# A two-layer graph attention kernel: fifteen-product thirds for the second products, seven-product aggregation for the last head and layer 2, and sums forked in PSUM

## The chip, the cores and the metric

The kernel runs on one core of a Trainium2 chip. Time is the device time of one execution in microseconds; lower is better. The engines have queues of their own: PE (TensorE, the matrix engine), DVE (VectorE), ACT (ScalarE), POOL (GpSimd) and SP (SyncE). SP issues plain transfers, POOL issues the transfers that add what they bring to what already lies in the destination; 16 DMA engines carry both. Each engine works through its queue in order and waits on semaphores of the others.

## The reference, cut to what matters

512 nodes, 768 features, 16896 edges with both directions and the self loops; layer 1 has 8 heads of 768 features, layer 2 has one head.

```python
h = (x @ W).reshape(n, H, C)                     # W1: 768 x 6144, W2: 6144 x 768
e = leaky_relu(alpha_s[src] + alpha_d[dst], 0.2)  # alpha = <h, a>
e = exp(e - max over dst); alpha = e / (sum over dst + 1e-16)
out = segment_sum(h[src] * alpha)                 # concatenated over heads, + b
...
h = elu(gat_layer(x, W1, ...)); out = gat_layer(h, W2, ...)
return layernorm(x + out)
```

The kernel writes the edges as a dense 512 x 512 matrix of counts. A head of layer 1 is then three dense products in fp32: the projection hs = x W1[:, head] (512 x 768 x 768), the aggregation gT = elu((PT hs) + b) (512 x 512 x 768, PT being the normalised attention), and the second product, which adds g W2[head] (512 x 768 x 768) into h2, the layer-2 features. After the eighth head come layer 2's attention, its aggregation of h2 and the norm.

## The kernel before, in words

**Products.** One `nc.tensor.matmul` has a 128 x 128 weight and a moving operand of up to 512 columns; in fp32 it is two PE instructions. The kernel saves PE work with block schemes that need fewer products than the plain method and pay for it with additions on DVE:

- Seven products for a 2 x 2 x 2 split (`left`, `right`, `projection`, `second`): 42 matmuls of 384 columns for a projection or a second product. `mixed` does the same for an aggregation: 42 matmuls of 256 columns.
- Fifteen products for a 2 x 3 x 3 split (`by_thirds`, with `load_thirds` and `x_thirds` for the operands): 60 matmuls of 256 columns. Before the change only the projections of heads 3 to 7 use it.

The sums of the left operand are made on DVE (`gsums`, `left_sums`, `x_thirds`), those of the right operand partly on DVE, partly by transfers of the POOL queue with `accum_op=ALU.add`.

**Stages.** The loop `for h in range(H - 1)` runs, in this order: `mixed(h)` (aggregation and elu of head h), `second(h)`, and the projection of head h + 2. The attention scores of head h + 1 (`lift`, `leak`, `rank`, `weigh`, `turn_out`, `turn_in`) are worked in between the products of `second(h)`. The last head is aggregated plainly, by `aggregate`: 24 matmuls of 512 columns. Layer 2 is aggregated plainly too, in the last loop: for each block of 128 nodes 4 matmuls of each column group, with the norm of a block done while the next one is multiplied.

**Order.** The program keeps the order in which the Python calls are written. So what stands where in each engine's queue is set by these loops by hand: `pairs[n][0]()` multiplies, `pairs[n][1]()` empties the PSUM bank, and sums and scores are called between them. PSUM: five banks in a ring `mm` (`Ring`), two for transposes, one for broadcasts.

**Loads.** W1[h + 2] goes to the buffers named `w2...` at the head of the loop body. W2[h + 1] goes to the buffers named `w1...` at the end of `second(h)`, right behind `reload_x()`, which brings five sums of x back from DRAM:

```python
if not last and n == 6:
    turn_out(q[3], 3, weigh(q[3], 3, scale=False))
    if 0 < h:
        sums = rest_of_thirds()
        reload_x()
    load_w2(h + 1)()
```

`load_w2` loads t1 (half of the upper rows), adds the other half to it, loads six blocks of rows, and adds the lower right block to the upper right one; the DVE sums from it (lines 384 and 385) come after the last product of the following projection.

Of the kernel before, what the change touches and what calls it, by code (L numbers as in the profile page):

```python
# [18 lines left out]
EPS_DEN = 1e-16  # L19
# [18 lines left out]
def gat_pass(  # L38
# [56 lines left out]

    mm, held = Ring(banks[:3]), Ring(banks[3:])
# [22 lines left out]
    def load_w(W, h, slot, m):  # L119


        t1 = wpool.tile([P, HK, HALF], F32, name=f"{slot}t1")
        upper = m[:HK * P, :].rearrange("(k p) d -> p k d", p=P)
        nc.sync.dma_start(t1, upper[:, :, L])
        nc.gpsimd.dma_start(t1, upper[:, :, R], accum_op=ALU.add)
        if slot == "w2":
            rows_ = wpool.tile([P, DC, D], F32, name="w2r")
            W[h] = [rows_[:, :HK], rows_[:, HK:], t1]
        else:
            W[h] = [wpool.tile([P, HK, D], F32, name=f"{slot}{r}") for r in range(2)] + [t1]  # L130
        for k in range(DC):
            nc.sync.dma_start(W[h][k // HK][:, k % HK, :], m[k * P:(k + 1) * P, :])

        def rest():

            nc.gpsimd.dma_start(W[h][0][:, :, R], m[HK * P:, R].rearrange("(k p) d -> p k d", p=P),
                                accum_op=ALU.add)
        return rest
# [3 lines left out]
    def third(rows_, k, n):  # L142
        return rows_[:, 2 * k:2 * k + 2, n * TH:(n + 1) * TH]

# [3 lines left out]
    def load_thirds(h):  # L148

        m = w1[:, h * D:(h + 1) * D]  # L150

        def part(k, n):
            return m[k * TH:(k + 1) * TH, n * TH:(n + 1) * TH].rearrange("(k p) d -> p k d", p=P)

        def flat(j):
            return wpool.tile([P, HK, HALF], F32, name=f"w2t{j}").rearrange("p k n -> p (k n)")

        rows_, pair_ = wpool.tile([P, DC, D], F32, name="w2r"), flat(1)
        add = ALU.add
        for k in range(DC):  # L160
# [8 lines left out]
        raw = {(k, n): third(rows_, k, n) for k in range(3) for n in range(3)}  # L169
# [33 lines left out]
    W1[0] = [wpool.tile([P, HK, D], F32, name=f"w1{r}") for r in range(2)]  # L203
# [231 lines left out]
    def by_thirds(h, A_, B_):  # L435

        HS[h] = hs = hpool.tile([P, NT, D], F32, name="hs")
# [6 lines left out]
        def step(p, chain, o, how):  # L444
# [9 lines left out]
            def empty():  # L454
# [3 lines left out]
                else:  # L458
                    nc.vector.tensor_tensor(out(o), out(o), ps, op=how)  # L459
            return multiply, empty  # L460

        plus, minus = ALU.add, ALU.subtract
        return [step(*a) for a in (
# [4 lines left out]
            ("P3", "y", (0, 2), -1.0))]  # L468

    def second(h, A_, B_):  # L470
# [3 lines left out]
        def pair(p, i, start, acc, new):  # L474
            def multiply(between=None):
                if start:
                    bank[i] = mm.next()
                product(bank[i], A_, B_, p, i, start, between)

            def empty():  # L480
                a, ps = acc(i), bank[i][:, :HALF]
                if new and h == 0 and p in ("P1", "P2"):
                    nc.scalar.copy(a, ps)
                elif new and (h == 0 or h == H - 1 and p == "P1"):
                    nc.vector.tensor_scalar(a, ps, -1.0 if p == "P7" else 1.0, None, op0=ALU.mult)
                else:
                    nc.vector.tensor_tensor(a, a, ps, op=ALU.subtract if p == "P7" else ALU.add)  # L487
            return multiply, empty

        steps = [  # L490
            ("P1", True, lambda i: u2[:, i, :], True),
            ("P2", False, lambda i: h2[:, i, L], True),
            ("P6", True, lambda i: u2[:, i, :], False),
            ("P7", True, lambda i: h2[:, 2 + i, R], True),
            ("P4", False, lambda i: h2[:, 2 + i, L], True),
            ("P5", True, lambda i: h2[:, 2 + i, R], False),
            ("P3", False, lambda i: h2[:, i, R], True),
        ]
        return [pair(p, i, *rest) for p, *rest in steps for i in range(2)]
# [13 lines left out]
    nb1T = const.tile([P, H * DC], F32, name="nb1T")  # L513

# [98 lines left out]
    def turn_b1():  # L613
# [3 lines left out]
        nc.scalar.activation(nb1T, psb[:, :H * DC], AF.Copy, scale=-1.0)  # L617

# [9 lines left out]
    if not general:  # L628
# [35 lines left out]
        def digits():  # L664

            whole = ohp.tile([P, NT, SW], I32, name="whole")
            nc.vector.tensor_scalar(whole, sums[:, :NT * SW].rearrange("p (t c) -> p t c", c=SW), float(1 << 24), None,
                                    op0=ALU.min)
            for d in range(N // SW):
# [3 lines left out]
                else:  # L673
                    nc.vector.tensor_scalar(o, whole, 3 * d, None, op0=ALU.logical_shift_right)

# [4 lines left out]
        s1, s2, s3, s4 = xsums  # L680
        m = lambda n: items[n][0]()
        e = lambda n: items[n][1]()
        hot = [f for q_ in range(NT) for f in one_hots(q_)]

        def some_hot(n):
            for f in hot[:n]:
                f()
            del hot[:n]

        some_hot(3)  # L690
        m(0)
        turn_x(2, 0)
        turn_x(3, 0)
        e(0)
        e(1)
        turn_x(2, 1)
        turn_x(3, 1)
        m(2)
        m(3)
        some_hot(2)  # L700
        s1()
        B1 = weight_sums()
        e(2)
        s2()
        e(3)
        s4()
        some_hot(1)
        m(4)
        m(5)
        e(4)  # L710
        wsums[0]()
        m(6)
        e(5)
        m(7)
        e(6)
        e(7)
        s3()
        some_hot(3)
        count((0, 1))
        m(8)  # L720
        some_hot(1)
        m(9)
        e(8)
        wsums[1]()
        e(9)
        turn_b1()
        m(10)
        m(11)
        some_hot(1)
        e(10)  # L730
        some_hot(1)
        e(11)
        m(12)
        halves = [half_logits(0, t) for t in range(NT)]
        ours, theirs = ([p_[j] for p_ in halves] for j in range(2))
        for f in (ours[0], theirs[0], ours[1]):
            f()
        count((2, 3))
        m(13)
        digits()  # L740
        e(12)
        e(13)
        ours[2]()
        for t in range(2):
            logarithm(t, counts)
        ours[3]()
        pairs = first_projection(1, XA, B1, lambda: spread(0))
        pairs[0][0]()
        masks(0)
        fold_count(0)  # L750
        q = [lift(0, 0)]
        theirs[1]()
        for t in range(2, NT):
            logarithm(t, counts)
        warm = small.tile([P, 1], F32, name="warm")
        nc.scalar.activation(warm, tiny, AF.Exp)
        q.append(lift(0, 1))
        for n in (0, 1):
            pairs[n][1]()
        for t in (2, 3):  # L760
            theirs[t]()
            q.append(lift(0, t))
    else:
# [28 lines left out]
        q = [lift(0, t) for t in range(NT)]  # L792
# [11 lines left out]
    def weigh(q, t, scale=True):  # L804
# [3 lines left out]
        nc.vector.tensor_scalar(rden, den, EPS_DEN, None, op0=ALU.add)  # L808
# [50 lines left out]
    def left_sums(h):  # L859
        hs = HS[h]  # L860
        a11, a12, a21, a22 = hs[:, :2, L], hs[:, 2:, L], hs[:, :2, R], hs[:, 2:, R]
        s1, s2, s4 = (gS.rearrange("p a k n -> p a (k n)")[:, j, :].rearrange("p (k n) -> p k n", k=2)
# [20 lines left out]
    def mixed(h, A_, B_, fill):  # L883

        tt = nc.vector.tensor_tensor
        behind = []

        def some(n):
            for f in fill[:n]:
                f()  # L890
            del fill[:n]

        for c in range(HK):
            u = work.tile([P, HN], F32, name="u")
            w = work.tile([P, HN], F32, name="w")
            zr = work.tile([P, N], F32, name="zr", bufs=3)
            bank = {}

            def part(p, over=None):
                if over is None:  # L900
                    bank[p] = mm.next()
                else:
                    bank[p] = bank[over]
                for k in range(2):
                    nc.tensor.matmul(bank[p][:, :HN], A_[p][:, k, c * P:(c + 1) * P], B_[p][:, k, :],  # L905
                                     start=over is None and k == 0, stop=k == 1, skip_group_check=True)
                return bank[p][:, :HN]

            nc.scalar.copy(u, part("P1"))  # L909
            if behind:  # L910

                behind = behind[0]()
            tt(u, u, part("P6"), op=ALU.add)
            tt(w, u, part("P7"), op=ALU.add)
            for f in behind[:1]:
                f()
            near_l = elu(h, c, part("P2", over="P1"), near, "l")
            some(1)
            tt(zr[:, far_], part("P5"), w, op=ALU.subtract)
            for f in behind[1:]:  # L920
                f()
            tt(zr[:, near], u, part("P4", over="P7"), op=ALU.add)
            near_l()
            tt(u, part("P3", over="P5"), u, op=ALU.subtract)
            some(-(-len(fill) // (2 * (HK - c) - 1)))
# [413 lines left out]
```

## Time and profile before

| | |
|---|---|
| median of 3 runs | 631.49 us (631.09 to 631.51) |
| the profiled execution | 631.3 us, of which the span from first to last instruction is 629.5 us |
| PE busy | 620.2 us (99%) |
| DVE busy | 491.1 us (78%) |
| ACT busy | 289.1 us (46%) |
| POOL busy | 62.2 us (10%) |
| granted TensorE clock | 0.998 |
| moved by DMA | 107.49 MB |

A row of the groups gives the line of the kernel, the engine, the operation, output and inputs by tile name, the shapes, the count, then busy time and mean duration of one, then the idle time of the engine before these instructions and what ended it. A row of the chain in order of time gives start, length, engine, tile, line and count. PE durations overlap their neighbours; the chain's rows, length over count, give the distance from one start to the next. SP's and POOL's rows show when a transfer is issued; "us to landing" is from issue to landing.

### The profile page before, as it was taken

Reading aid. Unit: us, or ns where it says so; the run is one execution under the profiler, and the core shown is the slowest. Engines: PE = TensorE matmul, PEld = TensorE weight load, DVE = VectorE, ACT = ScalarE, POOL = GpSimd, SP = SyncE. Lnnn points to the kernel's source line nnn. Section 1 sums busy time; section 2 is a strip of 40 time slices with the busy share of each in tenths; the row PEclk is TensorE's granted clock in tenths of the full one; section 3 lists DMA queues with packets and bytes.
Section 4 is the critical chain, followed back from the end, with each engine's and each line's share of the span. In section 5 each row is a group of like instructions: output and inputs, shape, how many; then the busy total and the mean of one; then the engine's idle time right before and its main releaser. Section 6 shows DMA issues by size and latency. Waiting matters only on the chain.

```text
span 629.5 us, 7475 instructions
## 1 busy us (share of the span) xinstructions
PE 620.2 (99%) x2509; PEld 435.5 (69%) x2509; DVE 491.1 (78%) x986; ACT 289.1 (46%) x511; POOL 62.2 (10%) x105
## 2 busy tenths in 40 slices
PE   9999999999999999999999999999999999999995
PEld 5665675558658885688758886688757886545553
DVE  8889878787887877777876878678876878676775
ACT  3138684703556073723546164722637054543540
POOL 1210110012001030020200130020200110000000
PEclk9999999999999999999999999999999999999999
DMA  8982978697708993398808884298808990500122
GB/s 286 319 175 68 254 235 213 151 252 217 187 17 248 226 238 112 72 334 228 208 11 225 220 233 152 52 333 232 223 0 205 293 264 18 159 0 1 33 59 79
DMA packets 85753, 107.49 MB, mean 171 GB/s; under 512 B 40086, under 2 KB 67150, under 8 KB 84942
## 3 DMA queue, kind: packets, MB, share of 16 engines
q1 hardware_dynamic: 69790, 86.24, 42.8%
q0 software_dynamic: 15488, 20.12, 19.3%
q10 hardware_dynamic: 432, 0.59, 0.3%
q8 instruction: 22, 0.36, 0.2%
q14 instruction: 21, 0.17, 0.1%
HBM read 93.94 MB, written 2.90 MB: 154 GB/s over the span
## 4 chain that ended last, share of the span: by engine, by line
PE 94%; DVE 3%; ACT 1%; issue 0%; DVEq 0%
PE mm L392 43%; PE mm L451 21%; PE mm L905 20%; PE mm L851 3%; PE mm L1285 3%; PE bc L656 1%; PE mm L561 1%; PE bc L248 1%; PE mm L279 1%; DVE scr L401 0%; DVE q L593 0%; DVE cnt L611 0%; DVE hs L541 0%; DVE q L598 0%; PE tr L1209 0%
## 5 line engine op out<-in xcount | busy, mean ns | idle before, releaser
L392 PE MATMUL mm<-w,gT 128*128 128x384 f32 x252 | 83.6, 486 | 0.0
L392 PEld LDWEIGHTS mm<-w,gT 128*128 128x128 f32 x252 | 47.9, 190 | 31.9
L601 ACT ACTIVATE q<-q,nmax 128x512 f32<-128x512 f32 x36 | 26.0, 723 | 92.6 <-DVE nmax L598 92.6
L487 DVE TENSOR_TENSOR h<-h,mm 128x384 f32<-128x384 f32 x72 | 39.2, 552 | 31.0 <-PE mm L392 30.6
L905 PE MATMUL mm<-PT,hs 128*128 128x256 f32 x252 | 61.4, 379 | 0.0
L392 PE MATMUL mm<-w1t,gS 128*128 128x384 f32 x180 | 60.5, 486 | 0.0
L457 ACT ACTIVATE hs<-mm 128x512 f32<-128x512 f32 x30 | 17.9, 596 | 89.9 <-PE mm L451 71.8
L905 PEld LDWEIGHTS mm<-PT,hs 128*128 128x128 f32 x252 | 47.8, 190 | 6.7
L392 PEld LDWEIGHTS mm<-w1t,gS 128*128 128x128 f32 x180 | 34.2, 190 | 23.9
L459 DVE TENSOR_TENSOR hs<-hs,mm 128x512 f32<-128x512 f32 x45 | 30.8, 685 | 22.9 <-PE mm L451 22.9
L905 PE MATMUL mm<-pS,gS 128*128 128x256 f32 x168 | 43.1, 379 | 0.0
L833 ACT COPY PT<-zr 128x1024 uint16<-128x1024 uint16 x34 | 39.3, 1157 | 3.4 <-DMA zr<-pS 3.3
L451 PE MATMUL mm<-w2r,xT 128*128 128x256 f32 x160 | 37.8, 379 | 0.0
L451 PE MATMUL mm<-w2r,gT 128*128 128x256 f32 x160 | 37.5, 382 | 0.0
L905 PEld LDWEIGHTS mm<-pS,gS 128*128 128x128 f32 x168 | 31.9, 190 | 4.3
L451 PEld LDWEIGHTS mm<-w2r,gT 128*128 128x128 f32 x160 | 30.0, 190 | 5.8 <-DVE hs L459 1.9
L451 PEld LDWEIGHTS mm<-w2r,xT 128*128 128x128 f32 x160 | 30.4, 190 | 5.2
L392 PE MATMUL mm<-w1t,gT 128*128 128x384 f32 x96 | 32.4, 487 | 0.0
L909 ACT COPY u<-mm 128x256 f32<-128x256 f32 x21 | 7.8, 372 | 47.6 <-PE mm L905 47.6
L392 PE MATMUL mm<-w,gS 128*128 128x384 f32 x84 | 28.6, 486 | 0.0
L451 PE MATMUL mm<-w2t,xS 128*128 128x256 f32 x120 | 27.5, 379 | 0.0
L828 ACT COPY pS<-q 128x1024 uint16<-128x1024 uint16 x26 | 27.2, 1044 | 0.7
(233 smaller groups left out, 1197.3 us busy)
## 6 DMA issues: line engine op xcount, KB each, us to landing
w2r<-in_L_gnn_W_dram SPq DMA_DIRECT2D x48, 384.0 KB, 7.2
w<-in_L_gnn_W_dram SPq DMA_DIRECT2D x43, 384.0 KB, 11.8
gT<-xd SPq DMA_DIRECT2D x5, 1280.0 KB
w<-in_L_gnn_W_dram POOLq DMA_DIRECT2D x8, 576.0 KB, 8.7
w1t<-in_L_gnn_W_dram SPq DMA_DIRECT2D x7, 576.0 KB
w1t<-in_L_gnn_W_dram POOLq DMA_DIRECT2D x7, 576.0 KB, 9.6
w2t<-in_L_gnn_W_dram SPq DMA_DIRECT2D x15, 256.0 KB, 7.3
w2t<-in_L_gnn_W_dram POOLq DMA_DIRECT2D x15, 256.0 KB, 9.2
```

Of the source, the lines that this page charges most:

```text
L392: nc.tensor.matmul(ps[:, :HALF], A_[p][:, k, i * P:(i + 1) * P], B_[p][:, k, :], start=start and k == 0, stop=k == HK - 1, skip_group_chec ...
L451: nc.tensor.matmul(bank[chain][:, i * TH:(i + 1) * TH], A_[p][:, k, i * P:(i + 1) * P], B_[p][:, k, :], start=first and i == k == 0, stop= ...
L457: nc.scalar.activation(out(o), ps, AF.Copy, scale=how)
L459: nc.vector.tensor_tensor(out(o), out(o), ps, op=how)
L487: nc.vector.tensor_tensor(a, a, ps, op=ALU.subtract if p == "P7" else ALU.add)
L601: nc.scalar.activation(q, q, AF.Exp, bias=nmax, scale=-1.0, accum_out=dens[t])
L828: nc.scalar.copy(apart.rearrange("p (h n) -> p h n", h=2), q.bitcast(U16).rearrange("p (n h) -> p h n", h=2))
L833: nc.scalar.copy(PT.rearrange("p s n -> p (s n)").bitcast(U16).rearrange("p (s n h) -> p s n h", s=NT, h=2)[:, :, t * P:(t + 1) * P, :], p ...
L851: nc.tensor.matmul(ps[:, :N], HS[h][:, s, c * P:(c + 1) * P], PT[:, s, :], start=(s == 0), stop=(s == NT - 1))
L905: nc.tensor.matmul(bank[p][:, :HN], A_[p][:, k, c * P:(c + 1) * P], B_[p][:, k, :], start=over is None and k == 0, stop=k == 1, skip_group ...
L909: nc.scalar.copy(u, part("P1"))
L1285: nc.tensor.matmul(ps[:, :cols.stop - cols.start], PT[:, s, t * P:(t + 1) * P], h2[:, s, cols], start=(s == 2), stop=(s == 1))
```

## The change

It replaces the hand-written loops by scripts: strings of operation names which `run(script, ops)` calls in the order written. `HEAD` covers `mixed`, `SECOND` the second product, `NEXT` the projection of head h + 2, `END` everything after the loop. In the names `m.`/`M.` multiplies, `e.`/`E.` empties a bank, `g.` is a sum of g, `w.` a sum of W2, `T.` a sum of W1. What is computed changes in these ways:

- The second products of heads 1 to 6 use the fifteen-product thirds (`second_thirds`, `g_thirds`): 60 matmuls of 256 columns in place of 42 of 384; 12 sums of g and 8 of W2 on DVE in place of 4 and 2; results of 128 x 512 emptied in place of 128 x 384.
- W2 of heads 1 to 6 is loaded by `load_thirds("w1", ..., True)`: six blocks of rows with two additions of 256 KB into them, two loads of 256 KB (P13, P12) with an addition each, and one more load and addition (P11). `apart=True` takes the row blocks in the order 1, 4, 2, 5, 0, 3. The sum `w.P2` = P12 - P13 needs both additions; it stands in `NEXT` between the eleventh product and its emptying.
- Head 2's projection uses `by_thirds` too; `x_thirds` is made during `second(0)`.
- `mixed` keeps its running sum in PSUM: after P1 ACT copies the bank into a second one (`fork`), P6, P7 and P4 are added there, and ACT keeps copies u and w of it on the way; P2 is added to the first bank. The biases are added in the copies, so that elu takes fewer operations. PSUM banks come from a list (`Free`) and go back to it by name.
- The last head is aggregated by `mixed` (42 matmuls of 256 columns), and its PE transposes (`turn`) go by DMA like the others.
- Layer 2 is aggregated by seven products (28 matmuls of 384 columns); the columns of all four node blocks are finished together and the four norms follow each other.
- b2 is added to x by POOL transfers rather than on DVE.

The diff, cut to its core:

```diff
+    class Free:
+        def __init__(self, tiles):
+            self.tiles = list(tiles)
+        def next(self):
+            return self.tiles.pop(0)
+        def release(self, tile_):
+            self.tiles.append(tile_)
...
-    def load_thirds(h):
+    def load_thirds(slot, m, apart):
...
+        order = [k for n in (range(3) if not apart else (1, 2, 0)) for k in of(chunks, n)]
+        for j, k in enumerate(order):
             nc.sync.dma_start(rows_[:, k, :], m[k * P:(k + 1) * P, :])
-            if k == 3:
-                nc.gpsimd.dma_start(third(rows_, 1, 1), part(1, 2), accum_op=add)
-            if k == 5:
-                nc.gpsimd.dma_start(third(rows_, 2, 1), part(0, 1), accum_op=add)
+            if j == (1 if apart else 3):
+                nc.gpsimd.dma_start(third(1, 1), part(1, 2), accum_op=add)
+            if j == (3 if apart else 5):
+                nc.gpsimd.dma_start(third(2, 1), part(0, 1), accum_op=add)
         for j, (k0, k1, n) in enumerate(((0, 2, 2), (0, 1, 0))):
             nc.sync.dma_start(square(pair_, j), part(k0, n))
             nc.gpsimd.dma_start(square(pair_, j), part(k1, n), accum_op=add)
...
+    def second_thirds(h, A_, B_):
+        bank, ops = {}, {}
+        def out(o):
+            return h2[:, 2 * o[0]:2 * o[0] + 2, o[1] * TH:(o[1] + 1) * TH]
+        def add(p, chain, o, how):
...
+            def multiply():
+                first = chain not in bank
+                if first:
+                    bank[chain] = mm.next()
+                for i in range(2):
+                    for k in range(2):
+                        nc.tensor.matmul(bank[chain][:, i * TH:(i + 1) * TH], A_[p][:, k, i * P:(i + 1) * P], B_[p][:, k, :],
+                                         start=first and i == k == 0, stop=k == 1, skip_group_check=True)
+            def empty():
+                ps = bank[chain].rearrange("p (i n) -> p i n", i=2)
+                if chain == "a":
+                    nc.scalar.copy(out(o), ps)
+                else:
+                    nc.vector.tensor_tensor(out(o), out(o), ps, op=how)
...
+    def run(script, ops):
+        for name in script.split():
+            ops.pop(name)()
...
+            def fork(st=st, j=far_j):
+                st["B"] = mm.next()
+                nc.scalar.activation(st["B"][:, :HN], st["A"][:, :HN], AF.Identity, bias=b1T[:, j:j + 1])
+            def keep_copy(name, st=st):
+                def f():
+                    st[name] = work.tile([P, HN], F32, name=name)
+                    nc.scalar.copy(st[name], st["B"][:, :HN])
...
+    HEAD = [...
+        """P10 P50 fork0 src0 P60 u0 P20 n0 src1 row P70 w0 x0 nn0 N0 P11 fork1 P40 b0 loads P30 y0 w.P0 B0 f0 dst0 P51 F0 P61
+        u1 P21 n1 w.P1 P71 w1 x1 nn1 dst1 N1 P12 fork2 P41 b1 P31 lift0 y1 f1 leak0 P52 B1 P62 u2 lift1 rank0 F1 g.P9 P22 n2
+        P72 w2 leak1 g.P12 x2 m.P2 nn2 rank1 N2 P42 b2 e.P2 g.P7 m.P9 P32 w.P4 B2 e.P9 y2 g.P1 f2 buffers""",
+    SECOND = [...
+        """g.P11 m.P12 lift2 e.P12 F2 g.P13 m.P1 lift3 out0 e.P1 m.P0 leak2 e.P0 m.P13 g.P10 rank2 out1 e.P13 seed m.P10 g.P6
+        e.P10 m.P4 leak3 rank3 e.P4 w.P3 m.P11 g.P8 e.P11 m.P6 g.P3 rest out2 g.P14 e.P6 m.P8 att0 w.P7 m.P14 e.P14 m.P3 att2
+        out3 g.P5 att1 in0 e.P3 m.P7 e.P7 m.P5 late e.P8 e.P5""",
+    END = """P10 fork0 ls0 P11 fork1 in2 P20 n0 nn0 P21 n1 N0 ls1 nn1 P12 fork2 N1 in3 P22 n2 r0 nn2 r1 P50 N2 P60 u0 r2 ...
+        ... m.P5.1 2in0 e.P5.0 2den3 2part3 2in1 m.P3.0 e.P5.1 m.P3.1 2in2 e.P3.0 fold4 2in3 f.P1.0 f.fork0 e.P3.1 fold5 f.P1.1 f.fork1 c0 a0 f.P2.0 c1 a1 f.P2.1 y11.0 c2 a2 y11.1
+        f.P5.0 f.P5.1 f.P6.0 xu0 c3 f.P6.1 xu1 f.P7.0 xw0 a3 f.P7.1 xw1 y22.0 f.P3.0 y22.1 f.P3.1 y12.0 f.P4.0 y12.1 norm0 f.P4.1 norm1 hint y21.0 norm2 y21.1 norm3"""
+    NEXT = [...
+        """M.P8 T.P6 T.P2 E.P8 M.P13 E.P13 T.P4 l0 in1 M.P9 E.P9 l1 in2 M.P2 E.P2 M.P4 T.P10 T.P0 E.P4 in3 M.P12 E.P12 l2 r0
+        M.P6 T.P1 l3 E.P6 M.P0 E.P0 M.P1 r1 E.P1 M.P10 r2 T.P7 E.P10 M.P5 r3 w.P2 E.P5 M.P14 src2 E.P14 w.P6 M.P11 E.P11 T.P3
+        M.P7 M.P3 E.P7 w.P10 src3 E.P3 dst3 dst2"""]
...
+        def late():
+            reload_x()
+            B_, more = load_thirds("w1", w2[(h + 1) * D:(h + 2) * D, :], True)
+            new.update(B=B_, W=more())
...
+    for t in range(NT):
+        nc.gpsimd.dma_start(xr[:, t, :], row_bcast(b2), accum_op=ALU.add)
...
+    def less_(i, t, cols):
+        return lambda: nc.vector.scalar_tensor_tensor(xr[:, t, cols], bank["B", i][:, :HALF], rden[t], xr[:, t, cols],
+                                                      op0=ALU.mult, op1=ALU.subtract)
+    def result(name, i, t, cols, op, free):
...
+            nc.vector.scalar_tensor_tensor(y[0][:, t, cols], bank[name, i][:, :HALF], rden[t], xr[:, t, cols],
+                                           op0=ALU.mult, op1=op)
...
+            nc.vector.bn_stats(stats[t][:, 0 if cols == L else 1, :], y[0][:, t, cols])
```

`y22`, `y12` and `y21` are calls of `result`, `xu` and `xw` of `less_`; `norm` is the chain bn_aggr, square root, reciprocal, offset, scaling and output transfer of one node block.

More of the change, by code (lines that the diff above doesn't have):

```diff
@@ L881, in right_sums @@
         ]
[L883 to L891, printed above, removed]
-        for c in range(HK):
[L894 to L925, printed above, removed]
-            def others(c=c, u=u, zr=zr):
-                return [elu(h, HK + c, zr, slice(0, N), "r", spare=zr), elu(h, c, u, far_, "l", spare=u)]
-            behind = [others]
-        return behind[0]()
@@ new lines, in final, with f, fork_ @@
+    def final(p, i, name):
+        def f():
+            start = (name, i) not in bank
+            if start:
+                bank[name, i] = mm.next()
+            for k in range(2):
+                nc.tensor.matmul(bank[name, i][:, :HALF], A2[p][:, k, i * P:(i + 1) * P], C2[p][:, k, :],
+                                 start=start and k == 0, stop=k == 1, skip_group_check=True)
+        return f
+    def fork_(i):
+        def f():
+            bank["B", i] = mm.next()
+            nc.scalar.copy(bank["B", i][:, :HALF], bank["A", i][:, :HALF])
+        return f
@@ L1309, in gat_pass, with hint @@
+    ops.update({f"norm{t}": norm(t) for t in range(NT)})
+    def hint():
+        if not general:
+            tc.mark_branch_hint_location("again", "LikelyTaken", [mybir.EngineType.Activation, mybir.EngineType.DVE, mybir.EngineType.SP])
+    ops["hint"] = hint
+    run(END, ops)
     return again
```

803 lines of the change are left out of this document (397 added, 406 removed).

## The prediction

> **What bounds the kernel now.** I read the page's totals first, then the chain in order of time, then busy time by stage, then the queues of SP and POOL around one W2 load.
>
> ```profile
> span 629.5 us, 7475 instructions
> PE 620.2 (99%) x2509; PEld 435.5 (69%) x2509; DVE 491.1 (78%) x986; ACT 289.1 (46%) x511; POOL 62.2 (10%) x105
> ...
> PE 94%; DVE 3%; ACT 1%; issue 0%; DVEq 0%
> ```
>
> The profiled execution took 631.3 us, 1.8 more than its span; the median of the runs is 631.49. I sum against 631.3. PE is the bound nearly everywhere, so a removed matmul is worth its distance to the next one. The chain in order of time gives that (start, length, count):
>
> ```profile
> 90.43 54.18 PE mm L392 x168
> ...
> 360.23 18.38 PE mm L905 x84
> 378.61 27.09 PE mm L392 x84
> 405.70 26.15 PE mm L451 x120
> ...
> 547.44 1.29 PE mm L392 x4
> 549.85 20.87 PE mm L851 x48
> ```
>
> One head of the loop is the three rows from 360.23: aggregation 18.38, second product by sevenths 27.09, projection by thirds 26.15. A fp32 matmul is two instructions: 27.09/84 = 0.3225 us each at 384 columns, 26.15/120 = 0.218 at 256. Busy time by stage of the same head (window; PE, PEld, DVE, ACT, POOL busy with counts; clock; DMA share; GB/s):
>
> ```profile
> 360.23:378.61 18.38, 18.38 (x85) 15.87 (x85) 13.58 (x31) 11.56 (x26) 4.88 (x4) 1.00 0.82 217
> 378.61:405.70 27.09, 27.09 (x85) 15.96 (x85) 20.82 (x47) 14.20 (x25) 0.00 (x0) 1.00 0.35 100
> 405.70:431.85 26.15, 26.15 (x121) 22.71 (x121) 21.14 (x35) 8.07 (x11) 3.76 (x3) 1.00 0.90 249
> ```
>
> PE has no gap; DVE is busy 55.5 of 71.6 us; the 16 DMA engines are 90% busy in the projection, the stage in which W2 arrives.
>
> **What PE gains.** (1) Six second products: 27.09 becomes 60 matmuls = 26.15, -0.94 each, -5.6. (2) Head 2's projection: the row of 168 is `second(0)` and this projection, 27.09 each, so -0.9. (3) The last head: 20.87 (48 instructions of 512 columns) becomes a `mixed`, 18.38: -2.5. Its first `far` product needs `in3`, and ACT has three forks, six copies of elu and two `in` ahead of that; I let PE wait 1.0 there (0 to 1.5): net -1.5. (4) The four PE transposes between 548.73 (547.44 + 1.29) and 549.85 go: -1.1. Sum: -9.1.
>
> **DVE.** It gets more work; is it the next bound?
>
> ```profile
> L459 DVE TENSOR_TENSOR hs<-hs,mm 128x512 f32<-128x512 f32 x45 | 30.8, 685 | 22.9 <-PE mm L451 22.9
> L487 DVE TENSOR_TENSOR h<-h,mm 128x384 f32<-128x384 f32 x72 | 39.2, 552 | 31.0 <-PE mm L392 30.6
> L384 DVE TENSOR_TENSOR w1t<-w1t,w 128x1152 f32<-128x1152 f32 x8 | 10.8, 1351 | 0.0
> L372 DVE TENSOR_TENSOR gS<-gT 128x768 f32<-128x768 f32 x8 | 7.7, 958 | 0.3
> L922 DVE TENSOR_TENSOR zr<-u,mm 128x256 f32<-128x256 f32 x21 | 8.8, 418 | 3.7 <-PE mm L905 3.1
> ```
>
> Per head: 14 results of 128x512 (the fifteenth is ACT's) for 14 of 128x384, +14 x 0.133 = 1.9; 12 sums of g for 4 of 128x768, 12 x 0.685 - 4 x 0.958 = +4.4; 8 sums of W2 for 2, 8 x 0.685 - 2 x 1.351 = +2.8; `mixed` gives nine operations of 128x256 to ACT or drops them, -9 x 0.418 = -3.8. Net +5.3: 60.8 of a head's 70.7, 86%. Spread over the three scripts it leaves every one under its PE time, so I cost it at nothing; what hides it is PE work with 10 us of room per head, and without that cover it would cost these 5.3 us for six heads.
>
> **Where a wait appears: `w.P2`.** It stands in DVE's queue behind the emptying of the tenth product and needs the additions to P12 and P13, the last things of the W2 load but one. The queues of SP and POOL in the head before:
>
> ```profile
> 334.50 1.23 SPq L830 DMA_TRANSPOSE zr<-pS  x1
> 336.20 1.23 SPq L830 DMA_TRANSPOSE zr<-nr  x1
> 337.60 0.46 SPq L177 DMA_DIRECT2D w2t<-in_L_gnn_W_dram  x1
> 338.11 0.47 SPq L962 DMA_DIRECT2D gT<-xd  x1
> ...
> 339.16 3.12 SPq L132 DMA_DIRECT2D w<-in_L_gnn_W_dram  x6
> ```
>
> ```profile
> 341.02 1.20 POOL L178 DMA_DIRECT2D w2t<-in_L_gnn_W_dram  x1 [37.97 <-DVE w2t L181]
> 346.37 1.28 POOL L125 DMA_DIRECT2D w1t<-in_L_gnn_W_dram  x1 [4.16 <-PE mm L451]
> 350.68 1.28 POOL L136 DMA_DIRECT2D w<-in_L_gnn_W_dram  x1 [3.02 <-DMA w<-in_L_gnn_W_dram]
> ```
>
> And the DMA view of 334 to 366 us (32 us):
>
> ```profile
> DMA  0097799999989999999999999999992000999999
> ...
> q1 hardware_dynamic: 4390, 6.51, 62.0%
> q0 software_dynamic: 1072, 1.44, 26.3%
> ...
> w<-in_L_gnn_W_dram POOLq DMA_DIRECT2D x1, 576.0 KB, 9.1
> w2t<-in_L_gnn_W_dram POOLq DMA_DIRECT2D x1, 256.0 KB, 8.8
> ```
>
> The engines are full from the reload on. SP's queue moved 6.51 MB in 0.62 x 32 = 19.8 us, 0.328 MB/us; POOL's adding queue 1.44 MB in 8.4 us, 0.171. Test: behind the reload (338.11) came 1280 + 576 + 2304 KB plain = 4.26 MB, 13.0 us, and 256 + 576 + 576 KB added = 1.44 MB, 8.4 us; sum 21.4. The last addition, issued at 350.68, landed 9.1 later, at 359.8: 21.7 behind the reload. The sum holds.
>
> After the change, from the reload to the addition to P12: plain 1280 (reload) + 2304 (rows) + 512 (P13, P12) + 256 (P11) KB = 4.46 MB, 13.6 us; added 5 x 256 KB = 1.31 MB, 7.7 us; 21.3. Less 0.7, since the addition of W1's P11 starts ahead of the reload; plus 1.0, since the last two additions can't start before their loads have landed: 21.6. The reload is issued about 0.4 behind the end of the second product: in SP's queue it stands behind W1's P11, which waits for `att1`, some 2.6 before that end (m.P7 and m.P5 still to come, less `att1`'s own work), and behind two transposes (1.23 each). So `w.P2` can start 22.0 us into the projection.
>
> When is it wanted? Ten products are 10 x 26.15/15 = 17.4; E.P10 and r3 bring DVE to 18.6. Behind `w.P2` DVE has E.P5, src2, E.P14, w.P6, E.P11 and T.P3, 4.6 us with it; the last product M.P3 waits for T.P3 and is due at 24.2. So the wait is free up to 24.2 - 4.6 = 19.6, and costs PE microsecond for microsecond beyond: 22.0 - 19.6 = 2.4, in six projections +14.4. Both ends: 0 if it lands by 19.6; 7.2 each if the last addition takes the 8.8 of the row above from a start at 18 (26.8), +43. I take 2.4: the packed sum was right to 0.3 us on the load of before. Queued behind the waiting `w.P2` are DVE's emptyings; PE waits for those two products later, over banks x and y, and the next head's DVE work starts no later against PE than without the wait.
>
> [...]
>
> **Layer 2 and the end.**
>
> ```profile
> 601.74 20.84 PE L1285 MATMUL mm<-h,PT 128*128 128x384 f32 x72
> ...
> 617.42 0.62 DVE L1289 SCALAR_TENSOR_TENSOR hs<-mm,rden,hs 128x384 f32<-128x384 f32 x1 [0.48 <-PE mm L1285]
> 618.07 0.56 DVE L1291 BATCH_NORM_STATS2 st<-hs 128x6 f32<-128x384 f32 x1
> ...
> 623.33 0.24 DVE L1295 BATCH_NORM_AGGREGATE mv<-st 128x2 f32<-128x18 f32 x1
> ...
> 624.20 0.47 DVE L1307 TENSOR_SCALAR hs<-hs,mv,rstd 128x384 f32<-128x384 f32 x1
> ```
>
> PE: 20.84 becomes 56 x 0.3225 = 18.1, -2.7. But f.P3.0 adds to the bank that `y22.0` reads, and DVE comes to `y22.0` only behind `xw1`, which waits for the product just before: two operations of 0.6, +1.2. Before, the last matmul ends at 622.6 and the last scaling at 624.67, 2.1 later. After, behind the last product DVE still has norm1, y21.0, norm2, y21.1 and norm3: a norm from aggregate to scaling is 624.67 - 623.33 = 1.34, a `y21` 0.62 + 0.56 less overlap = 1.1; 3 x 1.34 + 2 x 1.1 = 6.2, +4.1. Sum +2.6 (from -2.7, all hidden, to +4).
>
> **Sum.** 631.3 - 9.1 + 14.4 + 2.6 = 639.2, say 639.
>
> **Rivals.** (A) The load is in time: 631.3 - 9.1 + 2.6 = 624.8, faster. One mechanism: the additions land by 19.6. For it: the first 256 KB addition started into a full queue, these last two meet an emptying one. Against: 21.7 measured for nearly the same bytes. It decides at 20.7: a wait of 1.1 each, 6.5 in six, gives back all of the gain. [...] (B) It lands later still, 24.5: 4.9 each, 654; for it, 256-column blocks are shorter pieces than the 384-column ones measured. (C) The change does not do what it says on PE: 256-column products stall on their banks, since a chain of five goes through one bank and DVE is at 86%; with 0.5 us lost in each of six second products and seven aggregations and no late load, 631.5. Against: the thirds of before run at 0.218 with the same chains.
>
> **Chances.** The forecast (wait 1.2 to 4 us, 631 to 649) 0.50; A 0.30 (618 to 630); B 0.13 (649 to 665); C 0.07. The range 621 to 652 leaves out the ends of A and B. Less than 0.2% (1.3 us) cannot be told from no change. Faster: A and a little of C, 0.33; same 0.07; slower 0.60.
>
> **What would show it.** Each second product of heads 1 to 6 at 0.218 per instruction, 26.2 in all over its script; last head near 19.5. In each projection an idle stretch of DVE before the sum at line 197, ended by a DMA of P12 or P13, 22 us into it, and PE waiting on DVE before its last two products; projections of 28.5. At the end 6 us from last matmul to last scaling. If DVE does not wait at `w.P2`, or PE has gaps in `mixed`, the forecast is wrong in its mechanism.

## The result, and the profile after

The changed kernel takes 660.70 us (median of 4 runs, 658.97 to 663.89) against 631.29 (630.63 to 631.51): a ratio of 1.0473, 95% interval 1.0433 to 1.0514. It is slower, as forecast, but by 29 us and not by 8. The profiled execution, the fastest of the four, took 658.97 us with a span of 657.1; before it was 631.3 and 629.5.

The page of the changed kernel: span, busy times, TensorE's clock in 40 slices, and the shares of the chain that ended last.

```profile
span 657.1 us, 8223 instructions
...
PE 616.6 (94%) x2773; PEld 491.7 (75%) x2773; DVE 521.4 (79%) x1027; ACT 304.2 (46%) x557; POOL 90.5 (14%) x130
...
PEclk9999999999999899999999999999999899998997
...
PE 66%; DMA 15%; DVE 6%; ACT 5%; SPq 4%; issue 3%; POOL 0%; ACTq 0%; DVEq 0%; POOLq 0%
```

Before, the chain was PE for 94% and PE was busy for 99% of the span. Now 15% of the chain is DMA, PE has gaps, and in some slices its clock is no longer full. Where, the chain shows in order of time (start, length, what):

```profile
172.70 17.28 PE mm L545 x80
199.63 10.26 DMA w1t<-in_L_gnn_W_dram
211.19 6.12 DMA w1t<-in_L_gnn_W_dram
220.35 5.28 PE mm L468 x16
...
294.20 5.41 PE mm L468 x16
368.67 3.79 PE mm L468 x16
441.69 5.41 PE mm L468 x16
516.45 5.41 PE mm L468 x16
```

The second product by thirds is as forecast: 17.28/80 = 0.216 us per instruction, with no gap. Then the chain leaves PE for the loads of W2's pairs, in each of five heads. The last 16 matmuls of the projection follow, and here is something the forecast did not have: 16 instructions should take 16 x 0.216 = 3.5 us, and take 5.3 to 5.4 in four heads of five. The stretches of 3.4 us from those five starts (last columns: clock, DMA share, GB/s):

```profile
220.35:223.75 3.40, 3.40 (x9) 2.72 (x10) 1.75 (x3) 0.00 (x0) 0.00 (x0) 0.53 0.00 0
294.20:297.60 3.40, 3.40 (x10) 2.84 (x11) 2.28 (x4) 0.00 (x0) 0.00 (x0) 0.65 0.02 5
368.67:372.07 3.40, 3.40 (x15) 2.87 (x16) 3.11 (x6) 0.00 (x0) 0.00 (x0) 1.00 0.01 2
441.69:445.09 3.40, 3.40 (x9) 2.75 (x10) 1.74 (x3) 0.00 (x0) 0.00 (x0) 0.54 0.00 0
516.45:519.85 3.40, 3.40 (x9) 2.74 (x10) 1.92 (x4) 0.00 (x0) 0.00 (x0) 0.59 0.00 0
```

PE is busy throughout, and in four of the five its clock is half for most of that time: matmuls start 427 ns apart and not 216. In the third row, from 368.67, the clock is full. The waits of the changed kernel (total, times, longest):

```profile
DVE w1t L197 <- DMA w1t<-in_L_gnn_W_dram: 20.9, 6, 3.7
...
PE mm L468 <- DVE hs L476: 13.1, 5, 2.9
```

The first row is `w.P2`, six times, 3.5 us each; the second is PE behind it. VectorE at the end of one projection:

```profile
213.12 0.69 DVE L952 TENSOR_TENSOR pS<-pS,PT 128x512 f32<-128x512 f32 x1
217.41 0.69 DVE L197 TENSOR_TENSOR w1t<-w1t 128x512 f32<-128x512 f32 x1 [3.60 <-DMA w1t<-in_L_gnn_W_dram]
218.01 0.68 DVE L476 TENSOR_TENSOR hs<-hs,mm 128x512 f32<-128x512 f32 x1
218.73 0.96 DVE L418 SCALAR_TENSOR_TENSOR scr<-hs,a_s 128x768 bf16<-128x768 f32 x1
219.61 0.08 DVE L418 DVE_READ_ACCUMULATOR scr<-hs,a_s 128x1 f32 x1
219.61 0.68 DVE L476 TENSOR_TENSOR hs<-hs,mm 128x512 f32<-128x512 f32 x1
220.21 0.69 DVE L197 TENSOR_TENSOR w1t<-w1r 128x512 f32<-128x512 f32 x1
```

VectorE is free at 213.8 and waits until 217.4. Behind `w.P2` it empties P5, makes `src2` and empties P14 (219.61 to 220.29); at 220.35 PE starts M.P7, which adds to P14's bank.

The rest of the loss is in the last script. PE's instructions there that had to wait (in brackets the idle time ahead and what ended it):

```profile
572.49 1.13 PE L967 MATMUL mm<-PT,hs 128*128 128x256 f32 x4 [1.44 <-ACT mm L973]
574.29 2.86 PE L967 MATMUL mm<-pS,xS 128*128 128x256 f32 x12 [0.67 <-DVE pS L949]
...
579.68 1.10 PE L967 MATMUL mm<-pS,hs 128*128 128x256 f32 x4 [0.81 <-DVE pS L952]
...
594.86 3.52 PE L409 MATMUL mm<-w2r,gT 128*128 128x384 f32 x6 [2.27 <-ACT u L505]
...
613.01 2.20 PE L409 MATMUL mm<-w1t,gT 128*128 128x384 f32 x6 [0.54 <-DVE h L507]
...
639.98 2.85 PE L1323 MATMUL mm<-h,pS 128*128 128x384 f32 x8 [1.24 <-DVE hs L1341]
642.66 2.74 PE L1323 MATMUL mm<-xT,PT 128*128 128x384 f32 x8
```

Only the one at 639.98 was in the forecast. The row at 594.86 is six matmuls in 3.52 us, where six others of this shape take 2.20: the clock is halved there too. The last matmul ends at 645.4, 11.7 us ahead of the span's end (before: 622.6, 6.9 ahead).

An account of PE, worked out from the starts of all its matmuls: what lies between two starts beyond 216 ns at 256 columns, 323 at 384 and 430 at 512 is stall, the rest is work. Against a span of 629.5:

| us | forecast | found |
|---|---|---|
| PE's work | -12.8 | -14.6 (600.4 after, 615.0 before) |
| five projections: idle | +12.0 | +13.9 |
| the same: clock | 0 | +6.4 |
| head 2's projection: idle and clock | +2.4 | +4.4 and 1.5 |
| the last script: idle and clock | +2.2 | +8.8 and 1.7 |
| last matmul to the end | +4.1 | +4.8 |
| other stalls | 0 | +0.7 |
| sum | +7.9 | +27.6 |

### The profile page after: what moved, and what is told of

It is laid out like the page before. It is cut to its first block, busy times and chain, and to the rows that moved or that the text cites. A ratio compares the mean times of both kernels' runs of the same rounds, so it can differ in the third digit from the quotient of the medians.

```text
span 657.1 us, 8223 instructions
## 1 busy us (share of the span) xinstructions
PE 616.6 (94%) x2773; PEld 491.7 (75%) x2773; DVE 521.4 (79%) x1027; ACT 304.2 (46%) x557; POOL 90.5 (14%) x130
## 4 chain that ended last, share of the span: by engine, by line
PE 66%; DMA 15%; DVE 6%; ACT 5%; SPq 4%; issue 3%; POOL 0%; ACTq 0%; DVEq 0%; POOLq 0%
PE mm L967 20%; PE mm L545 19%; PE mm L409 15%; DMA w1t<-in_L_gnn_W_dram 12%; PE mm L468 7%; PE mm L1323 2%; SPq L177 2%; DMA hs<-in_x_dram 1%; ACT PT L904 1%; DVE hs L476 1%; PE bc L776 1%; DMA w2t<-in_L_gnn_W_dram 1%; ACT nr L899 1%; PE mm L653 1%; SPq L901 1%
## 5 line engine op out<-in xcount | busy, mean ns | idle before, releaser
L474 ACT ACTIVATE hs<-mm 128x512 f32<-128x512 f32 x36 | 21.5, 597 | 147.0 <-PE mm L468 146.4
L553 DVE TENSOR_TENSOR h<-h,mm 128x512 f32<-128x512 f32 x84 | 57.2, 681 | 13.0 <-PE mm L545 12.5
L468 PE MATMUL mm<-w2r,gT 128*128 128x256 f32 x192 | 52.5, 429 | 13.1 <-DVE hs L476 13.1
L468 PEld LDWEIGHTS mm<-w2r,gT 128*128 128x128 f32 x192 | 41.4, 218 | 22.3 <-DVE hs L476 15.1
L545 PE MATMUL mm<-w1r,gT 128*128 128x256 f32 x240 | 54.7, 379 | 0.0
L545 PEld LDWEIGHTS mm<-w1r,gT 128*128 128x128 f32 x240 | 45.5, 190 | 6.3
L896 ACT ACTIVATE q<-q,rden 128x512 f32<-128x512 f32 x28 | 20.1, 718 | 37.3 <-DVE rden L880 37.3
L545 PE MATMUL mm<-w1t,gT 128*128 128x256 f32 x144 | 34.1, 380 | 0.0
L545 PE MATMUL mm<-w1t,gS 128*128 128x256 f32 x144 | 34.0, 379 | 0.0
L418 DVE SCALAR_TENSOR_TENSOR scr<-hs,a_s 128x768 bf16<-128x768 f32 x32 | 30.6, 956 | 1.2
L418 DVE SCALAR_TENSOR_TENSOR scr<-hs,a_d 128x768 bf16<-128x768 f32 x32 | 30.5, 953 | 0.5
L545 PEld LDWEIGHTS mm<-w1t,gT 128*128 128x128 f32 x144 | 27.2, 190 | 4.1 <-DVE gT L579 0.4
```

The costliest lines, as they stand in the source:

```text
L418: return [lambda al=al, a=a, sign=sign: nc.vector.scalar_tensor_tensor(scr, HS[h][:, t, :], sign, a, op0=ALU.mult, op1=ALU.mult, accum_out ...
L468: nc.tensor.matmul(bank[chain][:, i * TH:(i + 1) * TH], A_[p][:, k, i * P:(i + 1) * P], B_[p][:, k, :], start=first and i == k == 0, stop= ...
L474: nc.scalar.activation(out(o), ps, AF.Copy, scale=how)
L545: nc.tensor.matmul(bank[chain][:, i * TH:(i + 1) * TH], A_[p][:, k, i * P:(i + 1) * P], B_[p][:, k, :], start=first and i == k == 0, stop= ...
L896: nc.scalar.activation(q, q, AF.Copy, scale=rden)
```

## Experiments

The reading to be tested has three parts. The additions to W2's pairs land when the bytes ahead of them have passed, and everything behind `w.P2` on VectorE waits for them. PE's idle time then halves its clock. And what is lost in the last script is lost to the order of the work. Rivals are named with each expectation. The kernel before, run beside these, took 631.0 to 631.2.

### The sum for P2 made one stage later

```diff
-  ... M.P10 r2 T.P7 E.P10 M.P5 r3 w.P2 E.P5 M.P14 src2 E.P14 w.P6 M.P11 ...     (NEXT)
+  ... M.P10 r2 T.P7 E.P10 M.P5 r3 E.P5 M.P14 src2 E.P14 w.P6 M.P11 ...
-  ... P30 y0 w.P0 B0 f0 ...                                                      (HEAD)
+  ... P30 y0 w.P2 w.P0 B0 f0 ...
```

> The sum for P2 is taken out of the projection and made in the next head's aggregation, ahead of the sum for P0. Theory (the wait for the addition to P12, and the halved clock that follows the idle time): the five idle stretches of PE at the ends of the projections of heads 3 to 7 (2.9, 2.3, 2.8, 2.9, 3.0 us over the floor, 13.9 together) and the slow matmuls behind four of them (about 6.5 us) go, the wait of head 2's projection for W1's own block stays: 659.0 - 20.4 = 638.6. Rival 1, the slow matmuls have another cause than the idle time: 659.0 - 13.9 = 645, with 427 ns matmuls still at the projections' ends. Rival 2, the wait only moves to the next thing that needs the load: within 3 us of 659.

Measured: 640.32 us (638.70 to 641.12), ratio 1.0136 (1.0118 to 1.0154) to the kernel before. Against 660.70 this is the 20.4 of the theory, to the digit by luck: between the two profiled executions it is 17.9, since a wait in head 2 grew. No projection of heads 3 to 7 has a stall or a matmul at 427 ns left. One wait grew, the one in head 2's projection:

```profile
PE mm L468 <- DMA w2t<-in_L_gnn_W_dram: 6.3, 1, 6.3
```

In the changed kernel this row was 4.3 us. It is another load: W1's block for P11.

### TensorE kept busy while it waits

```diff
-  w.P6 M.P11 E.P11 T.P3 M.P7 M.P3 ...
+  w.P6 M.P11 warm E.P11 T.P3 M.P7 M.P3 ...
+  warm: 10 x  matmul(spare[:, :128], ident, ident)    (15 more ahead of M.P11 in head 2's)
```

> The wait stays, but TensorE is given matmuls without use while it lasts: ten fp32 products of 128 columns into a spare bank ahead of the product that waits (2.2 us), and fifteen more (3.2 us) in head 2's projection. Theory (idle time halves the clock): the 38 or so matmuls at 427 ns behind the six waits run at 216, 8.0 us less, 651; the waits themselves stay as long. Rival, the clock is halved by something else, the load on the other engines or the DMA traffic: 659, and the rows at 427 ns stay.

Measured: 656.40 us (654.33 to 660.66), 4.3 less than the changed kernel. PE (line 1163 is the filling) and the wait of `w.P2`:

```profile
218.31 2.39 PE L1163 MATMUL bc<-ident 128*128 128x128 f32 x20
221.63 3.79 PE L468 MATMUL mm<-w2r,gT 128*128 128x256 f32 x16 [0.92 <-DVE hs L476]
```

```profile
DVE w1t L197 <- DMA w1t<-in_L_gnn_W_dram: 23.0, 6, 4.1
```

The 16 matmuls behind the wait take 3.79 and not 5.28 us, and none of the six projections has a slow one: with VectorE, the queues and the load as before and PE kept busy, the granted clock of this trace is 0.994, for 0.979 in the changed kernel. So the idle time is the cause here. This trace is of the fastest of the four runs; their granted clocks were 0.994, 0.994, 0.988 and 0.986, so two of them had more halved time than this one, in places that no trace shows.

The gain is 4.3 and not 8.0. By the starts of the matmuls, what PE spends waiting and filling ahead of the six products grew from 18.3 to 22.3 us. Of these 4.0, 1.7 lie in heads 3 to 7, where `w.P2` waits longer (the 23.0 above, for 20.9, is of all six), and 2.3 in head 2's projection: its second filling, 20 instructions from 146.15 to 148.38, stands where PE had nothing to wait for.

### The pairs' additions made later

```diff
+        if apart:
+            nc.sync.dma_start(square(four_, 0), part(0, 1))
+            nc.gpsimd.dma_start(square(four_, 0), part(1, 1), accum_op=add)
         for j, (k0, k1, n) in enumerate(((0, 2, 2), (0, 1, 0))):
             nc.sync.dma_start(square(pair_, j), part(k0, n))
             nc.gpsimd.dma_start(square(pair_, j), part(k1, n), accum_op=add)
```

> W2's block for P11 (256 KB plain and 256 KB added) goes ahead of the pairs P13 and P12 instead of behind them. Theory (the additions land when the bytes ahead of them have passed, 0.328 MB/us plain and 0.171 added): P12's addition lands 0.8 + 1.5 = 2.3 us later, the five waits of heads 3 to 7 grow from 2.8 to about 5.1, +11.5 us: 670.5; the slow matmuls stay as they are. Rival, the additions are held by something other than the bytes ahead of them (the start of each, its own load): the landing moves by less than 0.8 and the time stays within 4 us of 659.

Measured: 674.02 us (672.82 to 674.92), 13.3 more than the changed kernel. The wait of `w.P2` (line 202 here):

```profile
DVE w1t L202 <- DMA w1t<-in_L_gnn_W_dram: 31.3, 6, 6.1
```

It grew by 10.4 in six, 1.7 each, where the packed queues give 2.3. P12's addition lands 23.4 to 24.6 us into the projections of heads 3 to 7; in the changed kernel it was 21.5 to 22.3. PE's stalls ahead of M.P7 grew by 8.9 in the five projections (4.2, 4.4, 4.2, 4.6, 5.4). The addition follows what is put ahead of it, a quarter less steeply than the sum says. The rest of the 13.3 is mostly clock, where the theory had none: the projection that had escaped (368.67 above) now has slow matmuls too, and two others have more of them.

### The pairs loaded ahead of the row blocks

```diff
+        if apart: pairs_()                      # the two pair loads and their additions
         for j, k in enumerate(order):
             nc.sync.dma_start(rows_[:, k, :], m[k * P:(k + 1) * P, :])
```

> W2's pairs P13 and P12 with their additions go ahead of the row blocks instead of behind them; all else stays. Theory: their additions land some 8 us earlier and the sum for P2 waits for nothing; the additions to the row blocks land 2 to 4 us later, at 22 to 24 us into the projection, and the sum for P6, wanted some 1.5 us after the one for P2, waits 0.5 to 2.5 us instead: 640 to 650. Rival, the load is late as a whole and its order makes no difference: 657 to 660. Rival, the additions collide with the reload at the front and everything is later: over 662.

Measured: 642.75 us (642.49 to 643.17), ratio 1.0184 (1.0167 to 1.0201).

```profile
DVE w1t L202 <- DMA w1t<-in_L_gnn_W_dram: 5.4, 6, 1.2
```

Not a byte less is loaded, and the waits of `w.P2` fall from 20.9 to 5.4. PE's stalls at the projections' ends are 0.7 us and below, and no clock is lost there. It was the place of these additions in the queue. Moving what waits and moving what is waited for come within 2.4 us of each other, and both leave head 2's wait (6.2 here).

The time lies in the range of the theory, but not by its mechanism. The addition that `w.P2` waits for, and `w.P2` itself, in head 3:

```profile
208.39 9.57 DMA w1t<-in_L_gnn_W_dram
```

```profile
218.06 0.69 DVE L202 TENSOR_TENSOR w1t<-w1t 128x512 f32<-128x512 f32 x1 [1.23 <-DMA w1t<-in_L_gnn_W_dram]
```

P12's addition lands 18.9 to 19.8 us into the five projections: 2.6 earlier on average than in the changed kernel, not 8. So `w.P2` still waits, and the sum for P6, which was to wait in its place, waits only twice, 1.2 us in all. In the changed kernel and in these two runs the five additions of a load land in the order of POOL's queue, the first 17.1 to 18.2 us into the projection whichever it is, each of the others 1.2 to 2.7 later (mostly 1.3). P12's landing goes with its place among the additions (second here, fourth in the changed kernel, fifth in the run before this one). That a transfer lands when the bytes issued ahead of it have passed does not hold here: by that sum it would have landed near 14.

### W1's block ahead of W2's load in head 0

On top of the later sum:

```diff
-  ... X.11 X.12 X.13 late e.P3.1 rest X.7        (SECOND[0])
+  ... X.11 X.12 X.13 rest late e.P3.1 X.7
```

> As the run with the later sum for P2, and in head 0's second product the load of W1's block for P11 is issued ahead of W2's load instead of behind it. Theory (the 6.4 us wait in head 2's projection is this block, which stands behind 4.4 MB of W2): the wait and the slow matmuls behind it go, 640.3 - 8 = 632.5, about the time before. Rival, the queue is full there anyway and the block or W2 lands as late: 638 to 641.

Measured: 631.46 us (630.99 to 632.61, 10 runs), ratio 1.0007 (0.9997 to 1.0017): equal to the kernel before. No projection now waits for a load. Its heads follow each other at 69.9 us (from 145.50 to 215.43; 71.6 before), so the gain of the products by thirds is there, and the last script consumes it.

### The last script in another order

On top of that, with no work added or removed:

```diff
-  P10 fork0 ls0 P11 fork1 in2 P20 n0 nn0 P21 n1 N0 ls1 nn1 P12 fork2 N1 in3 P22 n2 r0 nn2 r1 P50 ...
+  P10 in2 fork0 ls0 P11 fork1 in3 P20 n0 nn0 P21 P12 fork2 r0 r1 N0 P60 P22 n1 r2 nn1 r3 u0 ...
-  m.P1.0 P42 b2 B2 m.P1.1 P32 y2 f2 ld0 e.P1.0 e.P1.1 F2 ...
+  m.P1.0 P42 b2 B2 ld1 e.P1.0 m.P1.1 P32 y2 e.P1.1 f2 F2 ...
-  f.P7.0 xw0 a3 f.P7.1 xw1 y22.0 f.P3.0 y22.1 f.P3.1 y12.0 f.P4.0 y12.1 norm0 f.P4.1 norm1 hint y21.0 norm2 y21.1 norm3
+  f.P7.0 xw0 y22.0 f.P7.1 f.P3.0 xw1 y22.1 f.P3.1 y12.0 f.P4.0 na0 y12.1 f.P4.1 na1 nb0 hint y21.0 nb1 na2 y21.1 nb2 na3 nb3
...
```

> As the run before in this list, with the order of the last script changed and no work taken out of it: the two late blocks of the attention matrix are copied ahead of the elu of the last head, its sums straight behind; layer 2's dot products fill idle time of VectorE; P1 of the last second product is copied ahead of the last elu; the first y22 stands ahead of the second xw; the four norms are cut in two and interleaved; and the six folds of head 0 are spread over head 2's projection. Theory (what the end lost is order, not the form with seven products): the stalls of 1.6, 0.8, 1.0, 2.4 with 1.7 of slow clock, 0.7, 0.8 and 1.4 us go for the most part, -8, the six folds -1, and the end behind the last matmul is 4 shorter: 632.5 - 13 = 619.5. Rival, VectorE and ScalarE are full there and the stalls come back at the next step: 627 to 633.

Measured: 622.96 us (622.76 to 623.70), ratio 0.9868 (0.9851 to 0.9884): 8.5 less than without. PE's stalls over the whole span fall from 18.2 to 10.3 us, the 8 of the theory. The end behind the last matmul is 10.3 in place of 11.7, so of the 4 expected there 1.4 came: a norm goes from VectorE to ScalarE and back, and VectorE still has two results of 1.1 us each to make behind the last product. One stall came back: the two last products of the last head wait 1.20 us where they did not before.

```profile
588.29 4.14 PE L409 MATMUL mm<-w2r,gS 128*128 128x384 f32 x12 [1.20 <-DVE rden L879]
```

### Layer 2 aggregated directly

Once on the kernel of 631.46, with its last script otherwise as changed, and once on the kernel of 622.96:

```diff
-  f.P1.0 f.fork0 e.P3.1 fold5 f.P1.1 f.fork1 c0 a0 ... y21.1 norm3
+  e.P3.1 fold5 direct hint
+  direct: per token block t and column group: 4 matmuls over (2, 3, 0, 1), scale, statistics; norm of t
```

> As the first run of this list, with layer 2's aggregation made directly again (72 matmuls in the order of the kernel before, each output block scaled and normalised as it comes) in place of the seven products. Theory (layer 2 in seven products, as it is ordered in the changed kernel, costs more at its end than it takes off TensorE): PE +2.7, the 1.4 and 0.5 us of waits for y22 go, last matmul to end of the span 6.9 in place of 11.7: 632.5 - 4 = 628.5. My forecast had it at 2.6: 630. Rival, the form itself gains: 634 to 636.

> As the run with the last script in another order, with layer 2's aggregation made directly as in the kernel before. From the first product of layer 2 to the end of the span the other run takes 29.6 us (seven products) and the run with the direct form 27.5. Theory (also when ordered well, the seven products lose at the end more than the 1.5 us of PE that they save): 623.0 - 2.1 = 620.9. Rival, the direct form waits for the late rows of the attention matrix, which the seven products read last: 623 to 625.

Measured: 627.73 us (626.99 to 628.20) and 621.55 us (621.03 to 621.91), 3.7 and 1.4 less than with seven products. In both orders the 72 instructions of the direct form beat the 56. What remains in a better order is the end behind the last matmul.

### The fourth sum of the last head's output earlier

On top of the last: the operation `g.3` (0.95 us on VectorE) moved from behind `fold1` to behind `e.P6.1`.

> As the run before in this list, with the fourth sum of the last head's output (an operation of 0.95 us) made 13 us earlier, out of VectorE's way ahead of the emptying that the last two products wait for. Theory: the 1.37 us stall there goes: 619.6. Rival, the emptyings behind its new place come later and the stall moves: 620.5 to 622.

Measured: 621.45 us (621.07 to 621.74), ratio 0.9847 (0.9831 to 0.9864), the same time as without. The stall went from 1.36 to 1.17, so the rival holds: the emptyings behind the new place come 0.3 us later, though PE itself is 0.4 earlier there, and VectorE reaches the one that PE waits for only 0.56 earlier. Together these edits make a kernel 1.5% faster than the one before.

### Idle times of six lengths

On the kernel of 631.46:

```diff
-  M.P7 M.P3 E.P7 ...
+  M.P7 hold M.P3 E.P7 ...
+  hold: matmuls into a spare bank; n x scalar.copy(t, ...) of 128x512; matmul(spare, ident, t)     n = 1 to 6
```

> On the kernel without late loads, TensorE is made to wait ahead of the last product of each of the six projections for a chain of 1, 2, 3, 4, 5 and 6 copies of 128x512 on ScalarE (about 0.6 us each) between two small products of no use. Theory (an idle time of some 2.3 us or more halves the clock for about 3.3 us behind it): the waits of about 0.9 and 1.5 us leave the matmuls behind them at 216 ns, those of 2.7, 3.3 and 3.9 are followed by 7 or 8 at 427 ns, and the one of 2.1 is open; the time is 631.5 + 6 x 1.1 for the small products + 14.4 of waits + 3 x 1.6 = 657. Rival, the halving hangs on the place in the program (what DVE and the DMA engines do there) and not on the length: slow matmuls behind short waits too, or behind none of them.

Measured: 661.35 us (one run). PE's idle time in the six projections (from start to start, less the 0.11 that a product of 128 columns takes): 0.84, 1.49, 2.14, 2.79, 3.44, 4.10 us. The 3.4 us behind each:

```profile
144.60:148.00 3.40, 3.40 (x17) 3.05 (x18) 3.08 (x7) 0.82 (x2) 0.00 (x0) 1.00 0.14 21
217.25:220.65 3.40, 3.40 (x17) 3.05 (x18) 2.46 (x5) 0.89 (x2) 0.00 (x0) 1.00 0.00 0
290.55:293.95 3.40, 3.40 (x11) 2.81 (x12) 1.28 (x4) 0.00 (x0) 0.00 (x0) 0.61 0.01 2
366.17:369.57 3.40, 3.40 (x10) 2.77 (x11) 0.67 (x2) 0.00 (x0) 0.00 (x0) 0.53 0.00 0
442.45:445.85 3.40, 3.40 (x9) 2.86 (x10) 0.01 (x2) 0.00 (x0) 0.00 (x0) 0.50 0.01 2
520.56:523.96 3.40, 3.40 (x10) 2.89 (x11) 0.00 (x0) 0.00 (x0) 0.00 (x0) 0.59 0.00 0
```

Full clock behind 0.84 and 1.49, about half behind all four from 2.14 on, with 6 to 12 matmuls at 427 ns (more where the wait was 3.44, where it cost 2.5 us, fewest behind 4.10). The place in the program is the same each time, so it is the idle time. These slow matmuls cost 7.2 us together, not the 4.8 of the theory, which explains half of the 4 us above its 657.

## Why the prediction was wrong

Its sign was right, and so was the wait that it put first. The size was off by 21.7 us in the medians (660.7 for 639.0), and 660.7 lies above its range: the wait was priced too low, and other waits were left out.

**Second products and PE.** "-0.94 each": right in kind, a little small. The second products run at 0.216 without a gap, and PE's work fell by 14.6 for a forecast of 12.8. VectorE's extra work is hidden, as costed: without the late loads the products of heads 1 to 6 wait for it once, for 0.4 us.

**`w.P2`, the landing.** Forecast 22.0 us into the projection. Read: the second product ends at 172.70 + 104 x 0.216 = 195.16, the addition to P12 lands at 211.19 + 6.12 = 217.31, 22.15 in (21.5 to 22.3 in the five heads). The packed sum of the two queues was right to 0.5. This was in part luck: the run with the pairs first shows that the sum does not tell where a transfer inside the load lands (near 14 by the sum, 18.9 to 19.8 read). P12's addition stands last but one in the load, where the sum of nearly all its bytes came out right.

**`w.P2`, the price.** "22.0 - 19.6 = 2.4, in six projections +14.4" is the step that failed first. Three things were wrong with it.
- It took the last product, M.P3, as the one that waits. It is M.P7, which comes earlier: it adds to the bank that E.P14 empties, and E.P14 stands behind `w.P2`. The idle time is 2.8 on average, 13.9 in five. This is a small error. (M.P3 itself is due at 14 x 26.15/15 = 24.4, not 24.2.)
- It ended the price with the wait. Behind four of these five idle times PE's clock was halved, for 3.41 us each, which cost another 6.4 us. Filling the wait shows that the idle time is the cause.
- The sixth projection, head 2's, was taken as like the others. That "the addition of W1's P11 starts ahead of the reload" holds in SECOND[1], where `rest` stands ahead of `late`. In SECOND[0] it stands behind, W1's block comes behind all of W2, and PE waits 4.4 us for it (6.4 with `w.P2` out of the way) and loses 1.5 to the clock. I costed the script by one of its variants.

Together these six projections cost 26.2 us by the account; undoing the two causes took off 20.4 and 8.9.

**Last head.** "I let PE wait 1.0": PE waits 1.4 for `fork2`, 0.7 and 0.8 for the sums of the attention matrix. The row of `in3` that I feared is not what it waits for first: ACT reaches `fork2` only behind `in2` and the elu of two blocks. And the second product of this head, costed at nothing, waits 2.3 us for the copy `e.P1.0` behind the last elu, with 1.7 of halved clock. ScalarE's queue ahead of that copy was not in my sum.

**Layer 2.** "-2.7, +1.2, +4.1": the wait of f.P3.0 is 1.24, last matmul to last scaling 6.7 (forecast 6.2), to the span's end +4.8. Taken out, layer 2's new form gives back 3.7 where the sum said 2.6. This step held.

**The rivals.** A (the load is in time) did not happen; with the waits undone the time is 631.5 and not its 624.8, since the last script loses what A counted as gained. B (654) is nearest in time, for another reason: the load is not later than forecast. C (631.5; its own terms add up to 631.3) did not happen: the products by thirds do not stall.

How much of the last script's loss belongs to the last head's aggregation in seven products alone was not run: its order was changed, its form was not undone.

## What to carry to other kernels

Price a wait by what stands behind it on its engine up to the first product whose bank it empties, and add the slow matmuls behind an idle TensorE: in heads 3 to 7 here the 13.9 us of waits brought 6.4 us of them. Cost a scripted order by every variant of the script: one variant had the load on the other side of 4.5 MB of transfers. If a load is late by a few microseconds, first move the operation that needs it, or the transfer's place in the queue; either took off 18 to 20 of the 29 us lost here without a byte less.

## What the hardware showed

In the run with six lengths, idle times of 0.84 and 1.49 us left TensorE's clock full; behind those of 2.14 us and more it was halved, with matmuls 427 ns apart in place of 216. In the trace of the changed kernel the clock was halved around the end of six idle times of PE, for 3.41 us each time (idle time from start to start, less 0.216):

| PE idle, us | next matmul at | clock halved |
|---|---|---|
| 4.45 | 144.01 | 145.03 to 148.44 |
| 2.92 | 220.35 | 220.12 to 223.53 |
| 2.26 | 294.20 | 295.21 to 298.63 |
| 2.91 | 441.69 | 441.99 to 445.40 |
| 3.04 | 516.45 | 517.08 to 520.49 |
| 2.43 | 594.86 | 595.59 to 599.00 |

The second of them in the profile (the first number behind the comma is PE's busy time, the third from the end the clock):

```profile
216.71:220.12 3.41, 0.88 (x5) 0.43 (x3) 2.68 (x5) 0.00 (x0) 0.00 (x0) 1.00 0.20 31
220.12:223.53 3.41, 3.18 (x8) 2.53 (x9) 1.98 (x4) 0.00 (x0) 0.00 (x0) 0.50 0.00 0
```

One idle time of 2.75 us (ahead of 368.67) went without, as did all the others between two matmuls of this trace, 1.61 us at most, from 5.1 us on, where its clock record begins. So the length of a wait does not settle it alone: 2.26 us was followed by the halving, and 2.75 was not. Nor does the place: the wait for `e.P1.0` in the last script (2.3 us in both) was followed by it in the changed kernel and not in the first run with layer 2 aggregated directly, where the clock is 0.9 or more in each of 40 slices but the last, and 0.997 in the mean. What else it hangs on, these runs do not show.
